# A graph layer on one core: 71 single rows per step for 40, and four edits to what the queues issue

## The chip, the cores and the metric

The kernel runs on one core of a Trainium2 chip. The metric is the time of one execution in device microseconds (us). The engines of a core run side by side and meet at semaphores: PE is the matrix engine (PEld is its loading of weights), DVE the vector engine, ACT the scalar engine, POOL the general one, and SP an engine that mostly starts DMA transfers. ACT and POOL start DMA transfers too. A name with a q (SPq, PEq) means the engine's sequencer: it waits, loads registers and issues transfers, and this is not counted as busy time. PE multiplies fp32 in two instructions, so one product of the program is two matmuls in the trace.

## The reference

There are 50,000 nodes with 128 numbers each, and 1,650,000 edges sorted by their destination. Every edge has a source, a destination and one of two types. An edge sends its source's row through the weights of its type; the messages are summed by destination; a product of the node's own row is added; then come a relu, a residual and a normalization over the 128 numbers.

```python
Xs = X[src]
m_data = Xs @ W_data.T + b_data
m_ctrl = Xs @ W_control.T + b_control
msg = jnp.where((edge_types == 0)[:, None], m_data, m_ctrl)
agg = jax.ops.segment_sum(msg, dst, num_segments=X.shape[0])
out = agg + (X @ W_self.T + b_self)
# of the whole:
x = _layernorm(x + jax.nn.relu(out), axis=-1)
```

Among the edges is one loop for every node, from the node to itself. Sum and product can change places, so the kernel first sums the source rows by destination and type and then multiplies the sums by the weights.

## The kernel before

**Blocks.** The edges are cut into blocks in their order. A block has Q = 2 steps. A step has R = 12 columns of 128 edges, whose source rows POOL fetches with one indirect DMA each (a *gather*, line 477); F = 42 *left-out* edges, which take the places of loops in those columns (a loop's row need not be fetched, since the node's own row is there anyway); and S = 40 *single rows*, which SP and ACT fetch with one plain transfer of 512 bytes each (`TURNS = (20, 20)`, SP's and ACT's share of a step). That makes 2 x (1,536 + 42 + 40) = 3,236 edges a block and NBLK = 510 blocks; the first and the last are "plain" and have neither left-out edges nor single rows. Ten blocks are a *group* (GB), whose lists of edge numbers are loaded together.

**Work for a block b**, in the order of the program's loop (lines 614 to 664). The loop goes through four *passes* (q = 0 to 3) of six columns each. The order on every engine is written out by hand; each engine works through its own instructions in this order and waits where a semaphore tells it to.

- `window(b + 3)` loads the transposed rows xT of a block's 112 destination nodes (line 406). Every BASES = 5 blocks SP loads five numbers into registers first (line 400): the first node of each block.
- `load_edges(g + 1)`, once a group: seven transfers on SP (lines 165, 170, 174).
- `products` (496): a pass waits until its six gathers have landed, then PE multiplies each 128 rows by a one-hot matrix oh. The gathers go into a ring of ten slots (`SLOTS`) of one pass each, so POOL may run ten passes ahead of PE and then waits for it (line 477).
- At the end of a step, `rows_fetched` makes PE wait (line 460, once a block, for both queues' semaphores) for the single rows of the block, and line 502 multiplies them. They lie in a ring of four blocks (`ROW_SLOTS`).
- `single_rows(b + 2, part)` issues the rows of the block after next, in two parts (q = 0 and 1). Each part first loads its 20 byte offsets into registers (`TENSOR_LOAD`, line 446), on SP and ACT each, and then issues 20 transfers (line 451), each after a MOVE of its register. The offsets are made by DVE in `offsets` (435).
- `add`, `begin_sums`, `moments`, `onehot` (412), `counts` (420), `fill` (lines 316 to 338) and `left_out_matrix` are DVE's part. `fill(b + 5)` puts left-out edges into the places of loops; `left_out_columns` (345) is PE's wait for it.
- `layer(b - 1)` (531 to 535) multiplies the finished sums by the weights; `moments`, `root` (ACT, 551), `store` (DVE, 557 and 559) and `store_rows` (SP, 563) normalize and write the block out.

Of the kernel before, what the change touches and what calls it, by code (L numbers as in the profile page):

```python
# [23 lines left out]
N = 50000  # L24
D = 128
ROW = 4 * D
E = 1650000
P = 128
# [8 lines left out]
Q = 2  # L37
PASS = 6
B = 112
C = R * Q  # L40
F = 42
TURNS = (20, 20)
S = sum(TURNS)
LOADS = 2
X = Q * S
R1 = R + 1
C1 = Q * R1
SIZES = [P] * R
SIZE = sum(SIZES)
CE = Q * SIZE  # L50
BE = CE + Q * F + X
NBLK = 2 + (E - CE) // BE
REST = E - CE - (NBLK - 2) * BE
REST_ROWS = [min(n, max(0, REST - q * SIZE - sum(SIZES[:r]))) for q in range(Q) for r, n in enumerate(SIZES)]
# [2 lines left out]
GB = 10  # L57
GROUPS = -(-NBLK // GB)
GC = GB * C1
# [17 lines left out]
assert NB * BLOCKS == N and G * BGROUPS == BLOCKS and (QB * P) % G == 0 and NCH < BIG  # L77
TBL = GROUPS * GB
GS = GB * Q


def plain(b):
# [5 lines left out]
    return bass.AP(tensor=ap.tensor, offset=ap.offset, ap=[[0, n], *ap.ap])  # L88


def straight(ctx, tc, c, x, x_t, src_t, dst_t, etype_t, src_f, dst_f, etype_f, src_x, dst_first, first_p, out):

# [20 lines left out]
    stp = ctx.enter_context(tc.tile_pool(name="stp", bufs=3))  # L113
# [5 lines left out]

    ctx.enter_context(tc.manual_schedule())  # L120
    idx0 = keep.tile([P, C1], I32, name="idx0")
    nc.sync.dma_start(idx0, src_t[:, :C1])


    num = keep.tile([P, 2 * W], F32, name="num")
# [5 lines left out]
    lists = [small[:, 2 * W + F + i * FILL:][:, :FILL] for i in range(2)]  # L131
# [7 lines left out]
                            base=0, channel_multiplier=-1)  # L139
# [11 lines left out]
    bias = keep.tile([3, D], F32, name="bias")  # L151
# [3 lines left out]
    loads = {}  # L155
# [7 lines left out]
    def load_edges(g):  # L163
        t = eds.tile([1, GB * X], I32, name="one_g")
        nc.sync.dma_start(t, src_x[None, g * GB * X:(g + 1) * GB * X])
        one_g[g] = t
        loads[g] = {}
# [224 lines left out]
    bys, pcs, zs, pls, bases, ats, ys = {}, {}, {}, {}, {}, {}, {}  # L392
    ohs, cnts, accs, xTs, pos, hs, mvs, sds, os_ = {}, {}, {}, {}, {}, {}, {}, {}, {}

    BASES = 5

    def window(b):
        if b % BASES == 0:
            n = min(BASES, NBLK - b)
            _, regs = nc.values_load_multi_w_load_instructions(  # L400
                base_i[0:1, b:b + n], engines=[SP], min_val=0, max_val=N - B,
                skip_runtime_bounds_check_because="it was clamped to this")
            bases.update({b + i: at for i, at in enumerate(regs)})
        at = bases[b]
        xT = stp.tile([P, B], F32, name="xT", bufs=5)
        nc.sync.dma_start(xT, x_t[:, bass.ds(at, B)])  # L406
        xTs[b] = xT

    def onehot(b):
# [20 lines left out]
    def offsets(b):  # L430

        if not plain(b):
            g, i = divmod(b, GB)
            ats[b] = stp.tile([1, X], I32, name="at_x", bufs=AHEAD + 2)
            nc.vector.tensor_scalar(ats[b], one_g[g][:, i * X:(i + 1) * X], float(ROW), None, op0=ALU.mult)

    def single_rows(b, part):

        if part == 0:
            ys[b] = stp.tile([S, Q, D], F32, name="yx", bufs=ROW_SLOTS)  # L440
        both = []
        for j, (eng, dma) in enumerate(((SP, nc.sync), (ACT, nc.scalar))):
            n = Q * TURNS[j]
            k0, k1 = part * n // LOADS, (part + 1) * n // LOADS
            at = Q * sum(TURNS[:j])
            _, rows = nc.values_load_multi_w_load_instructions(ats[b][0:1, at + k0:at + k1], engines=[eng], **RANGE)  # L446
            both.append([(dma, fetched[j][b % ROW_SLOTS], *divmod(k0 + k, TURNS[j]), sum(TURNS[:j]), row)
                         for k, row in enumerate(rows)])
        for pair in zip_longest(*both):
            for dma, sem, q, k, at, row in filter(None, pair):  # L450
                copy = dma.dma_start(ys[b][at + k:at + k + 1, q, :].bitcast(U8), x_bytes[:, bass.ds(row, ROW)])  # L451
# [84 lines left out]
        pos[b] = both  # L536

    def moments(b):
        h = stp.tile([B, D], F32, name="h")
# [5 lines left out]
        mv = stp.tile([B, 2], F32, name="mv")  # L545
        nc.vector.bn_aggr(mv, st)
        hs[b], mvs[b] = h, mv
# [6 lines left out]
    def store(b):  # L554
        mv = mvs.pop(b)
        rstd = stp.tile([B, 1], F32, name="rstd")
        nc.vector.reciprocal(rstd, sds.pop(b))
        o = stp.tile([B, D], F32, name="o")
        nc.vector.tensor_scalar(o, hs.pop(b), mv[:, 0:1], rstd, op0=ALU.subtract, op1=ALU.mult)
        os_[b] = o  # L560

    def store_rows(b):
        nc.sync.dma_start(out[bass.ds(bases.pop(b), B), :], os_.pop(b))  # L563

    def find_bad():

# [47 lines left out]
    for b in range(NBLK + 1):  # L614
        if b == NBLK - 1:
            find_bad()
        if b + 3 < NBLK:
            window(b + 3)
        g, i = divmod(b, GB)
        if i == 0 and g + 1 < GROUPS:  # L620
            load_edges(g + 1)
        if i == 3 and g + 1 < GROUPS:
            spread_out(g + 1)
        if i == 4 and g + 1 < GROUPS:
            spread_in(g + 1)
        if b > 0:
            add(b - 1, steps_of(b - 1)[-1])
        if b < NBLK:
            begin_sums(b)
        last = steps_of(b)[-1:]  # L630
        for q, (step, ks) in enumerate(passes_of(b)):
            if ks:
                products(b, step, ks)
            if q == 0 and b > 0:
                layer(b - 1)
            if q == 1:
                left_out_numbers(b + 1)
# [12 lines left out]
            if q == 1 and b + AHEAD < NBLK:  # L650
                counts(b + AHEAD)
            if q == 2 and i == 2 and g + 1 < GROUPS:
                columns(g + 1)
            if q == 2:
                left_out_rows(b + 1)
                if b + RAHEAD < NBLK:
                    fill(b + RAHEAD)
            if q == 3:
                left_out_matrix(b + RAHEAD)
                offsets(b + AHEAD + 1)  # L660
            if q < LOADS and not plain(b + AHEAD):
# [227 lines left out]
def gnn_resnorm(  # L889
# [1 line left out]
    tc: tile.TileContext,  # L891
    x: bass.AP,
    x_t: bass.AP,
    src_t: bass.AP,
    dst_t: bass.AP,
    etype_t: bass.AP,
    src_f: bass.AP,
    dst_f: bass.AP,
    etype_f: bass.AP,
    src_x: bass.AP,  # L900
    dst_first: bass.AP,
    first_p: bass.AP,
# [16 lines left out]
    nc = tc.nc  # L919
# [4 lines left out]
    eps = const.tile([P, 1], F32, name="eps")  # L924
# [13 lines left out]
             b_data=b_data, b_ctrl=b_ctrl, b_self=b_self)  # L938

    with ExitStack() as own:  # L940
        straight(own, tc, c, x, x_t, src_t, dst_t, etype_t, src_f, dst_f, etype_f, src_x,
                 dst_first, first_p, out)
# [10 lines left out]

# [47 lines left out]
```

## Time and profile before

| | |
|---|---|
| median of 12 runs | 18,933.21 us (18,862.37 to 18,952.98) |
| the profiled execution's own time | 18,966.55 us |
| its span, first to last instruction | 18,964.8 us |
| busy PE, DVE, POOL | 37%, 58%, 61% of the span |
| mean granted clock of PE | 0.598 |
| a gather on POOL (L477) | 944 ns busy, 12,216 and 24 of them |
| single rows on SP and on ACT (L451) | 20,320 each, 0.5 KB each |
| loads of offsets on SP (L446) | 1,016, median 1,198 ns |
| lists of a group on SP | 51 of each of seven, 3.1 to 130 KB |
| loads of matrix weights and matmuls of the single rows (L502) | 245 and 401 ns, 2,032 of each |

A line of the profile's groups reads: line, engine, operation, what it writes <- what it reads, shape, count | busy us, mean ns of one | idle time of the engine just before it, and what ended that. A line of the waits reads: who waited <- for whom: us in total, times, longest. A line of the timeline reads: start, duration, engine, line, operation, count, and in brackets the engine's idle time before it and what ended it; several of a kind in a row are merged. The view of one line of the program gives for each operation the count, the minimum, median and maximum in ns, and the first and last start. L451 is line 451 of the kernel before.

### The profile page before, as it was taken

The page shows a single profiled execution, that of the slowest core. Times are in us where ns is not written, and L with a number is a line of the kernel's source. Part 1 is how long each engine was busy: PE and PEld are TensorE (multiplying, and loading weights), DVE is VectorE, ACT ScalarE, POOL GpSimd, SP SyncE. Part 2 cuts the span into 40 slices and gives each one's busy share as a digit, 9 for nine tenths or more (in the row PEclk, how much of TensorE's full clock was granted, in tenths as well). Part 3 has the DMA queues.
Part 4 walks back from the last instruction along what each step waited for, and adds up shares of the span by engine and source line. Part 5 has one row for each costly group of instructions (what it writes and reads, how often), then busy time and mean ns, then how long its engine had stood idle before and what let it go on. Part 6 is the DMA issues. An engine that isn't in the chain of part 4 may idle for free. (4 is left out here: it accounts for less than half of the span.)

```text
span 18964.8 us, 197234 instructions
## 1 busy us (share of the span) xinstructions
PE 7104.0 (37%) x35844; PEld 6372.0 (34%) x35845; DVE 10926.6 (58%) x13994; ACT 153.5 (1%) x516; POOL 11559.9 (61%) x12250
## 2 busy tenths in 40 slices
PE   3333333333333333333333333334333333333333
PEld 2333333333333333333333333333333333333333
DVE  6555555555555555555555555555555555555554
ACT  0000000000000000000000000000000000000000
POOL 6665666656665666666666666665665666666665
PEclk6566556555655556565656565555566655566556
DMA  2211111111111211111111111111111111121111
GB/s 53 50 51 48 50 49 51 50 49 50 49 49 49 50 49 50 49 50 49 50 51 49 50 49 50 49 49 49 50 49 49 50 50 49 49 51 49 51 50 45
DMA packets 649294, 939.08 MB, mean 50 GB/s; under 512 B 327756, under 2 KB 445487, under 8 KB 648034
## 3 DMA queue, kind: packets, MB, share of 16 engines
q0 software_dynamic: 391680, 802.93, 16.8%
q1 hardware_dynamic: 215276, 112.76, 2.3%
q10 hardware_dynamic: 41078, 10.68, 0.2%
q14 instruction: 968, 7.93, 0.1%
q8 instruction: 292, 4.78, 0.1%
HBM read 895.92 MB, written 29.42 MB: 49 GB/s over the span
## 5 line engine op out<-in xcount | busy, mean ns | idle before, releaser
L477 POOL DMA_INDIRECT y<-in_x,idx x12216 | 11535.8, 944 | 7351.3 <-issue 3311.7
L496 PE MATMUL acc<-oh,y 128*128 128x120 f32 x24480 | 5044.2, 388 | 203.6 <-issue 202.4
L496 PEld LDWEIGHTS acc<-oh,y 128*128 128x128 f32 x24480 | 4774.7, 297 | 212.2 <-issue 211.7
L420 DVE TENSOR_REDUCE cnt<-oh 128x240 bf16<-128x3120 f32 x510 | 2966.9, 5818 | 0.1
L512 DVE TENSOR_TENSOR sums<-acc,sums 128x180 f32 x1020 | 352.8, 346 | 4354.2 <-PE acc L505 2086.7
L502 PE MATMUL acc<-oh,yx 40*128 40x120 f32 x2032 | 637.3, 401 | 4971.6 <-PEq L460 2960.0
L345 PE MATMUL small<-ones_b,by 128*84 128x1 bf16 x508 | 116.0, 228 | 6183.1 <-issue 3193.0
L345 PEld LDWEIGHTS <-by 128*84 128x84 bf16 x508 | 72.8, 143 | 6305.5 <-issue 3260.3
L502 PEld LDWEIGHTS acc<-oh,yx 40*128 40x128 f32 x2032 | 403.4, 245 | 5157.8 <-PEq L460 3010.8
L541 DVE COPY h<-po 112x128 f32<-112x128 f32 x510 | 148.7, 292 | 2847.3 <-remote 1410.1
L412 DVE TENSOR_TENSOR oh<-col,small 128x3120 f32<-128x3120 f32 x510 | 1719.3, 3371 | 0.0
L338 DVE TENSOR_REDUCE by<-old 128x84 bf16<-128x1092 f32 x508 | 1077.9, 2122 | 18.5 <-DVE old L335 0.9
L319 DVE TENSOR_TENSOR m<-rk,small 128x1092 f32<-128x1092 f32 x508 | 656.3, 1292 | 17.9 <-DVE small L317 0.7
L322 DVE TENSOR_TENSOR new<-m,small 128x1092 f32<-128x1092 f32 x508 | 656.1, 1291 | 17.4
L326 DVE TENSOR_REDUCE v_new<-new 128x26 f32<-128x1092 f32 x508 | 656.0, 1291 | 17.4
L335 DVE TENSOR_TENSOR old<-m,small 128x1092 f32<-128x1092 f32 x508 | 652.7, 1285 | 0.0
L535 PE MATMUL po<-wmsgT,sums 128*112 128x128 f32 x2040 | 520.5, 399 | 0.0
L535 PEld LDWEIGHTS po<-wmsgT,sums 128*112 128x112 f32 x2040 | 377.9, 255 | 108.8 <-issue 88.7
L533 PE MATMUL po<-bias,sums 3*112 3x128 f32 x1020 | 350.4, 439 | 99.4 <-DVE sums L512 64.3
L505 PE MATMUL acc<-cnt,to_row 128*128 128x60 bf16 x2040 | 272.2, 212 | 146.6 <-issue 146.1
L532 PE MATMUL po<-wselfT,xT 128*112 128x128 f32 x1020 | 313.8, 410 | 0.0
L525 DVE TENSOR_TENSOR sums<-pl,sums 128x336 f32<-128x336 f32 x508 | 258.0, 508 | 84.8 <-issue 70.9
(118 smaller groups left out, 4045.8 us busy)
## 6 DMA issues: line engine op xcount, KB each, us to landing
yx<-in_x ACTq DMA_DIRECT2D x20320, 0.5 KB
yx<-in_x SPq DMA_DIRECT2D x20320, 0.5 KB
y<-in_x,idx POOLq DMA_INDIRECT x12216
xT<-in_x_t SPq DMA_DIRECT2D x510, 56.0 KB
out<-o SPq DMA_DIRECT2D x510, 56.0 KB
vf_all<-vd SPq DMA_DIRECT2D x51, 420.0 KB
s<-in_src_t SPq DMA_DIRECT2D x51, 130.0 KB
d<-in_dst_t SPq DMA_DIRECT2D x51, 130.0 KB
```

Source lines behind the costliest of these rows:

```text
L319: nc.vector.tensor_tensor(m, rk_g[g][:, i, :, None].to_broadcast([P, C1, F]), rank_no_ps[:, None, :].to_broadcast([P, C1, F]), op=ALU.is_e ...
L322: nc.vector.tensor_tensor(new.rearrange("p (q r) f -> p q r f", r=R1), m.rearrange("p (q r) f -> p q r f", r=R1), vf.rearrange("p (q f) -> ...
L326: nc.vector.tensor_reduce(v, new, AX.X, ALU.add)
L335: nc.vector.tensor_tensor(old, m, cb[:, :, None].to_broadcast([P, C1, F]), op=ALU.mult)
L338: nc.vector.tensor_reduce(by, old.rearrange("p (q r) f -> p q f r", r=R1), AX.X, ALU.add)
L412: nc.vector.tensor_tensor(oh, col_g[g][:, i, :, None].to_broadcast([P, C1, 2 * W]), num_ps[:, None, :].to_broadcast([P, C1, 2 * W]), op=AL ...
L420: nc.vector.tensor_reduce(cnt, ohs[b].rearrange("p (q r) w -> p q w r", r=R1), AX.X, ALU.add)
L477: copy = nc.gpsimd.indirect_dma_start(out=y[:r, k % PASS, :].bitcast(U8), out_offset=None, in_=x_rows, in_offset=bass.IndirectOffsetOnAxis ...
L496: nc.tensor.matmul(acc[:, :2, :].rearrange("p t w -> p (t w)"), y[:r, k % PASS, :], ohs[b][:r, column(k), :], start=k == of_step[0], stop= ...
L502: nc.tensor.matmul(acc[:, :2, :].rearrange("p t w -> p (t w)"), ys[b][:, q, :], ohs[b][:S, q * R1 + R, :], start=False, stop=True)
L512: nc.vector.tensor_tensor(part, accs.pop((b, q)), part, op=ALU.add)
L535: nc.tensor.matmul(po, a[:, t, :B], c["wmsgT"][:, t * D:(t + 1) * D], start=False, stop=t == 1)
```

## The change

1. The single rows of a step go from 40 to 71, 35 on SP and 36 on ACT, and the left-out edges from 42 to 43. A block then has 3,300 edges. The offsets of a block are loaded in three parts of up to 32 registers for two parts of 20, issued at q = 0, 1 and 2; ACT's offsets start at a multiple of four.
2. The seven transfers of a group's lists become three: one list as before, the three lists of columns side by side in one tensor, and the three lists of left-out edges in another.
3. SP gets a block's byte offsets from DVE, which computes them once for all blocks before the loop, and no longer computes them from the node number for each transfer. The window's loads bring two numbers for each of four blocks.
4. ACT takes the root for two blocks at once; the stores of the two blocks follow it together.

```diff
-F = 42
-TURNS = (20, 20)
+F = 43
+TURNS = (35, 36)
 S = sum(TURNS)
-LOADS = 2
-X = Q * S
+LOADS = 3
+BEGIN = (0, -(-Q * TURNS[0] // 4) * 4)
+X = BEGIN[1] + -(-Q * TURNS[1] // 4) * 4
...
-BE = CE + Q * F + X
+BE = CE + Q * (F + S)
...
-        for name, a in (("s", src_t), ("d", dst_t), ("t", etype_t)):
-            t = eds.tile([P, GB, C1], I32, name=name, bufs=1)
-            nc.sync.dma_start(t.rearrange("p b c -> p (b c)"), a[:, g * GC:(g + 1) * GC])
-            loads[g][name] = t
-        for name, a in (("sf", src_f), ("df", dst_f), ("tf", etype_f)):
-            t = eds.tile([GS, F], I32, name=name, bufs=1)
-            nc.sync.dma_start(t, a[g * GS:(g + 1) * GS, :])
-            loads[g][name] = t
+        t = eds.tile([P, 3, GB, C1], I32, name="sdt", bufs=1)
+        nc.sync.dma_start(t.rearrange("p m b c -> p (m b c)"), edges_t[:, g * 3 * GC:(g + 1) * 3 * GC])
+        f = eds.tile([GS, 3, F], I32, name="sdt_f", bufs=1)
+        nc.sync.dma_start(f.rearrange("s m f -> s (m f)"), edges_f[g * GS:(g + 1) * GS, :])
+        loads[g] = {n: t[:, m] for m, n in enumerate("sdt")} | {n + "f": f[:, m] for m, n in enumerate("sdt")}
...
-    base_i = keep.tile([1, BL], I32, name="base_i")
-    nc.vector.tensor_copy(base_i, base[0:1, :, 0])
+    base_i = keep.tile([1, BL, 2], I32, name="base_i")
+    for i, size in enumerate((4, ROW)):
+        nc.vector.tensor_scalar(base_i[:, :, i], base[0:1, :, 0], float(size), None, op0=ALU.mult)
...
-    BASES = 5
+    BASES = 4
...
-        nc.sync.dma_start(xT, x_t[:, bass.ds(at, B)])
+        nc.sync.dma_start(xT.bitcast(U8), x_t_bytes[:, bass.ds(bases[b][0], 4 * B)])
...
+    def part_of(n, part):
+        return min(n, 32 * part)
...
-            k0, k1 = part * n // LOADS, (part + 1) * n // LOADS
-            at = Q * sum(TURNS[:j])
+            k0, k1 = part_of(n, part), part_of(n, part + 1)
+            at = BEGIN[j]
...
-    def root(b):
-        sd = stp.tile([B, 1], F32, name="sd")
-        nc.scalar.activation(sd, mvs[b][:, 1:2], AF.Sqrt, bias=c["eps"][:B, :])
-        sds[b] = sd
+    def pair(b):
+        return range(b // 2 * 2, b + 1) if b % 2 == 1 or b == NBLK - 1 else ()
+
+    def root(bs):
+        sd = stp.tile([B, 2], F32, name="sd")
+        nc.scalar.activation(sd[:, :len(bs)], mvs[bs[0] // 2][:, :len(bs), 1], AF.Sqrt, bias=c["eps"][:B, :])
+        sds[bs[0] // 2] = sd
...
+        for i, b in enumerate(bs):
+            o = stp.tile([B, D], F32, name="o", bufs=4)
+            nc.vector.tensor_scalar(o, hs.pop(b), mv[:, i, 0:1], rstd[:, i:i + 1], op0=ALU.subtract, op1=ALU.mult)
+            os_[b] = o
...
     def store_rows(b):
-        nc.sync.dma_start(out[bass.ds(bases.pop(b), B), :], os_.pop(b))
+        rows = out_bytes[bass.ds(bases.pop(b)[1], B * ROW)].rearrange("(p e) -> p e", e=ROW)
+        nc.sync.dma_start(rows, os_.pop(b).bitcast(U8))
...
-            if q == 1 and b > 0:
-                root(b - 1)
-            if q == 2 and b > 0:
-                store(b - 1)
+            if q == 1 and b > 0 and pair(b - 1):
+                root(pair(b - 1))
+            if q == 2 and b > 0 and pair(b - 1):
+                store(pair(b - 1))
...
             if q == 3 and b > 0:
-                store_rows(b - 1)
+                for done in pair(b - 1):
+                    store_rows(done)
```

More of the change, by code (lines that the diff above doesn't have):

```diff
@@ L79 @@
 GS = GB * Q
+CLAMPED = "it was clamped to this"
 def plain(b):
@@ L88, in row_bcast, with straight @@
     return bass.AP(tensor=ap.tensor, offset=ap.offset, ap=[[0, n], *ap.ap])
-def straight(ctx, tc, c, x, x_t, src_t, dst_t, etype_t, src_f, dst_f, etype_f, src_x, dst_first, first_p, out):
+def straight(ctx, tc, c, x, x_t, edges_t, edges_f, src_x, dst_first, first_p, out):
     nc = tc.nc
@@ L121, in straight @@
     idx0 = keep.tile([P, C1], I32, name="idx0")
-    nc.sync.dma_start(idx0, src_t[:, :C1])
+    nc.sync.dma_start(idx0, edges_t[:, :C1])
     num = keep.tile([P, 2 * W], F32, name="num")
@@ L166, in load_edges @@
         one_g[g] = t
-        loads[g] = {}
-        for name, a in (("s", src_t), ("d", dst_t), ("t", etype_t)):
-            t = eds.tile([P, GB, C1], I32, name=name, bufs=1)
-            nc.sync.dma_start(t.rearrange("p b c -> p (b c)"), a[:, g * GC:(g + 1) * GC])
-            loads[g][name] = t
-        for name, a in (("sf", src_f), ("df", dst_f), ("tf", etype_f)):
-            t = eds.tile([GS, F], I32, name=name, bufs=1)
-            nc.sync.dma_start(t, a[g * GS:(g + 1) * GS, :])
-            loads[g][name] = t
+        t = eds.tile([P, 3, GB, C1], I32, name="sdt", bufs=1)
[3 more added lines that the diff above has]
+        loads[g] = {n: t[:, m] for m, n in enumerate("sdt")} | {n + "f": f[:, m] for m, n in enumerate("sdt")}
     load_edges(0)
@@ L393, in straight @@
     ohs, cnts, accs, xTs, pos, hs, mvs, sds, os_ = {}, {}, {}, {}, {}, {}, {}, {}, {}
-    BASES = 5
+    BASES = 4
+    x_t_bytes = x_t.bitcast(U8)
+    out_bytes = out.rearrange("n d -> (n d)").bitcast(U8)
     def window(b):
@@ L400, in window @@
             _, regs = nc.values_load_multi_w_load_instructions(
[L401 to L404, printed above, removed]
+                base_i[0:1, b:b + n, :].rearrange("o b i -> o (b i)"), engines=[SP], min_val=0, max_val=(N - B) * ROW,
+                skip_runtime_bounds_check_because=CLAMPED)
+            for i in range(n):
+                at = nc.s_assert_within(regs[2 * i], 0, (N - B) * 4, skip_runtime_bounds_check_because=CLAMPED)
+                bases[b + i] = at, regs[2 * i + 1]
         xT = stp.tile([P, B], F32, name="xT", bufs=5)
-        nc.sync.dma_start(xT, x_t[:, bass.ds(at, B)])
+        nc.sync.dma_start(xT.bitcast(U8), x_t_bytes[:, bass.ds(bases[b][0], 4 * B)])
         xTs[b] = xT
@@ L538, in moments @@
     def moments(b):
-        h = stp.tile([B, D], F32, name="h")
+        h = stp.tile([B, D], F32, name="h", bufs=4)
         po = pos.pop(b)
@@ L544, in moments, with store @@
         nc.vector.bn_stats(st, h)
-        mv = stp.tile([B, 2], F32, name="mv")
+        if b % 2 == 0:
+            mvs[b // 2] = stp.tile([B, 2, 2], F32, name="mv")
+        mv = mvs[b // 2][:, b % 2, :]
         nc.vector.bn_aggr(mv, st)
-        hs[b], mvs[b] = h, mv
-    def root(b):
-        sd = stp.tile([B, 1], F32, name="sd")
-        nc.scalar.activation(sd, mvs[b][:, 1:2], AF.Sqrt, bias=c["eps"][:B, :])
-        sds[b] = sd
[L554 to L560, printed above, removed]
+        hs[b] = h
+    def pair(b):
[4 more added lines that the diff above has]
+        sds[bs[0] // 2] = sd
+    def store(bs):
+        mv = mvs.pop(bs[0] // 2)
+        rstd = stp.tile([B, 2], F32, name="rstd")
+        nc.vector.reciprocal(rstd[:, :len(bs)], sds.pop(bs[0] // 2)[:, :len(bs)])
+        for i, b in enumerate(bs):
+            o = stp.tile([B, D], F32, name="o", bufs=4)
+            nc.vector.tensor_scalar(o, hs.pop(b), mv[:, i, 0:1], rstd[:, i:i + 1], op0=ALU.subtract, op1=ALU.mult)
+            os_[b] = o
     def store_rows(b):
-        nc.sync.dma_start(out[bass.ds(bases.pop(b), B), :], os_.pop(b))
+        rows = out_bytes[bass.ds(bases.pop(b)[1], B * ROW)].rearrange("(p e) -> p e", e=ROW)
+        nc.sync.dma_start(rows, os_.pop(b).bitcast(U8))
     def find_bad():
@@ L893, in gnn_resnorm @@
     x_t: bass.AP,
[L894 to L899, printed above, removed]
+    edges_t: bass.AP,
+    edges_f: bass.AP,
     src_x: bass.AP,
@@ L940, in gnn_resnorm @@
     with ExitStack() as own:
-        straight(own, tc, c, x, x_t, src_t, dst_t, etype_t, src_f, dst_f, etype_f, src_x,
-                 dst_first, first_p, out)
+        straight(own, tc, c, x, x_t, edges_t, edges_f, src_x, dst_first, first_p, out)
     found = nc.values_load(bad, min_val=0, max_val=4 * P,
@@ L955 @@
     arrays = {k: np.ascontiguousarray(inputs[k], dtype=np.float32) for k in _FLOATS}
+    lists, fillers = [], []
     for k, pad in (("src", 0), ("dst", DST_PAD), ("edge_type_2", 0)):
@@ L975 @@
         single = steps[:, :, SIZE + F:]
-        ones[1:] = np.concatenate([single[:, :, sum(TURNS[:j]):][:, :, :n].reshape(TBL - 1, Q * n)
-                                   for j, n in enumerate(TURNS)], axis=1)
+        for j, n in enumerate(TURNS):
+            ones[1:, BEGIN[j]:BEGIN[j] + Q * n] = single[:, :, sum(TURNS[:j]):][:, :, :n].reshape(TBL - 1, Q * n)
         firsts = np.ascontiguousarray(cols[:, :, 0, 0])
-        arrays[k + "_t"] = np.ascontiguousarray(cols.reshape(TBL * C1, P).T)
-        arrays[k + "_f"] = fills.reshape(TBL * Q, F)
+        lists.append(cols.reshape(TBL * C1, P).T.reshape(P, GROUPS, GC))
+        fillers.append(fills.reshape(TBL * Q, F))
         if k == "src":
@@ L986 @@
             arrays["first_p"] = np.ascontiguousarray(both.transpose(2, 0, 1).reshape(GS, 2 * GROUPS))
+    arrays["edges_t"] = np.ascontiguousarray(np.stack(lists, axis=2).reshape(P, GROUPS * 3 * GC))
+    arrays["edges_f"] = np.ascontiguousarray(np.concatenate(fillers, axis=1))
     arrays["x_t"] = np.ascontiguousarray(arrays["x"].T)
@@ L993 @@
     with tile.TileContext(nc) as tc:
-        gnn_resnorm(tc, ap["x"], ap["x_t"], ap["src_t"], ap["dst_t"], ap["edge_type_2_t"], ap["src_f"], ap["dst_f"],
-                    ap["edge_type_2_f"], ap["src_x"], ap["dst_first"], ap["first_p"], ap["src"],
-                    ap["dst"], ap["edge_type_2"],
+        gnn_resnorm(tc, ap["x"], ap["x_t"], ap["edges_t"], ap["edges_f"], ap["src_x"], ap["dst_first"], ap["first_p"],
+                    ap["src"], ap["dst"], ap["edge_type_2"],
                     ap["L0_gnn_W_data"], ap["L0_gnn_b_data"], ap["L0_gnn_W_control"],
```

## The prediction

> **What bounds the kernel now.** I read the page first, then the waits of all engines, then SP's own waits, and last the timelines of SP, PE and POOL side by side. The page gives no engine as full:
>
> ```profile
> PE 7104.0 (37%) x35844; PEld 6372.0 (34%) x35845; DVE 10926.6 (58%) x13994; ACT 153.5 (1%) x516; POOL 11559.9 (61%) x12250
> ...
> L477 POOL DMA_INDIRECT y<-in_x,idx x12216 | 11535.8, 944 | 7351.3 <-issue 3311.7
> ...
> L502 PE MATMUL acc<-oh,yx 40*128 40x120 f32 x2032 | 637.3, 401 | 4971.6 <-PEq L460 2960.0
> ```
>
> POOL issues 24 gathers per block, one every 1.25 us (0.94 busy and 0.30 of issue), so 30.0 us of a block; a block takes 18,964.8 / 510 = 37.19 us. What holds POOL for the other 7 us is PE, through the ten slots of y, and PE itself sits in front of L502, the product with the single rows. The view of line 460 alone, PE's wait for those rows, has 508 waits with a median of 11.46 us. The waits of all engines say the same, and SP's own waits say who is late:
>
> ```profile
> PEld acc L502 <- PEq L460: 3010.8, 202, 26.0
> ...
> POOL y L477 <- PE acc L496: 1966.3, 410, 11.5
> ```
>
> ```profile
> SPq L446 <- DVE sums L512: 72.8, 74, 1.5
> SPq L301 <- DVE cb L279: 15.7, 1, 15.7
> SPq L563 <- DVE o L559: 11.1, 3, 6.8
> ```
>
> These are SP's three largest waits, 100 us in 18,965: SP is never out of work. It is not counted as busy, because issuing DMAs is not, but it is the full queue. The timeline of SP, with PE's for the same moment behind it:
>
> ```profile
> 8007.78 36.70 SPq L451 DMA_DIRECT2D yx<-in_x  x40
> 8044.74 0.34 SPq L563 DMA_DIRECT2D out<-o  x1
> 8045.32 0.36 SPq L406 DMA_DIRECT2D xT<-in_x_t  x1
> ...
> 8047.75 31.65 SPq L451 DMA_DIRECT2D yx<-in_x  x40
> ```
>
> ```profile
> 8045.55 0.50 PEld L502 LDWEIGHTS acc<-oh,yx 40*128 40x128 f32 x2 [10.52 <-PEq L460]
> ```
>
> SP ends its 40 rows at 8044.48, and PE goes on 1.1 us later after 10.52 us of waiting. Pairing every one of the 508 fences with the two queues, from the trace's records: 430 of them wait, and in all 430 SP's last row comes after ACT's, by more than a block and a half; the median from SP's last row to the end of the fence is 1.0 us. So SP's 40 rows bound the kernel, not POOL's gathers. ACT has the same 40 rows and room to spare.
>
> The price of a row is not constant, and this decides the sum. It depends on whether POOL is gathering:
>
> ```profile
> L451 SPq DMA_DIRECT2D yx<-in_x x7: 3/689/711, 8021.9 to 8031.1; - x7
> ```
>
> ```profile
> L451 SPq DMA_DIRECT2D yx<-in_x x21: 13/228/689, 11685.0 to 11694.3; - x21
> ```
>
> ```profile
> 11682.37 0.94 POOL L477 DMA_INDIRECT y<-in_x,idx  x1 [0.30 <-issue]
> 11694.85 0.94 POOL L477 DMA_INDIRECT y<-in_x,idx  x1 [11.53 <-PE acc L496]
> ```
>
> The columns are count and minimum, median, maximum in ns. Between 8021 and 8033 POOL gathers, ACT issues, and SP gets 7 rows out in 12 us. Between 11,685.5 and 11,694.5 POOL stands still for PE, and SP gets 21 rows out in 9 us. The timeline has a whole set of 40 at 11,691.70 in 16.00 us, against 36.70 above: 0.40 and 0.92 us a row, loads of the numbers included. The mean over all 508 sets is 31.5 us from first to last row, 0.79 a row; the other 5.7 us of SP's block are the first load, out, xT, the window's numbers and the lists.
>
> **The change part by part.** A block takes 3,300 edges for 3,236, so the blocks are 2 + 499 = 501 for 510, and the gathers 500 x 24 + 2 = 12,002 for 12,240. At POOL's own 1.25 us that is 297 us less, but POOL is not the bound, so alone it brings nothing.
>
> The single rows go from 40 to 70 per block on SP and from 40 to 72 on ACT. That is 30 rows more on the queue that is full. Bounds for one row: 0.40 us (the set at 11,691.70) and 0.92 (the set at 8007.78). I take 0.40, because the gathers of a block still take only 30.0 us: a block of before already lasts 37.19, so whatever is added to it is added while PE waits at L460, y's slots stay taken and POOL stands still, and that is the row measured in such a pause. 30 x 0.40 = 12.0 us. The loads are in it: before there are two loads of 20 registers per 40 rows, median 1.20 us each on SP, and after three of 32, 32 and 6 per 70.
>
> Taken from SP: four list transfers per ten blocks, medians 0.33 to 0.43 us, together 1.5 us or 0.15 per block; one register multiply each at L563 and L406, median 37 ns but 0.17 us in the mean of 510, together 0.34. Added: loads of the window's numbers, 8 registers every 4 blocks for 5 every 5, at 0.95 us each at least 0.05. I take -0.4; between the ends 0 and -0.6 it moves the total by 0.2 ms.
>
> Lying beside it: the left-out edges go from 42 to 43, so L319, L322, L326, L335 and L338 (7.28 us a block) grow by 1/42, 0.17 us on DVE; the offsets of L435 go from 80 to 144 numbers, 0.195 us now and at most 0.35 by length; the yx weights grow from 40 to 71 partitions, and L496 with 128 partitions takes 388 ns where L502 with 40 takes 401, so nothing on PE. The cover of all this is PE's wait at L460, 6,197 us in the 508 fences, 12.2 per block; without it 0.32 us x 501 would be 0.16 ms.
>
> The root for two blocks: ACT has one wait for mv fewer in two blocks, and where it remains it stands at the same place, with the second and third part of the rows of b+2 queued behind it, as before. The store of an even block moves one block later, past one set of SP's rows and one xT; its o and h have four buffers for it, and only the end of the program reads the output. DVE then makes two o in a row (0.40 us more in an odd block, that much less in an even one), ahead of the fill. On SP two out transfers follow each other, the number of them is the same on the mean. I cost this at nothing, under the same cover.
>
> Sum: 37.19 + 12.0 - 0.4 = 48.8 us; 501 x 48.8 = 24,450 us on the profiled span of 18,964.8 (its own time is 18,966.55). The last block has 2 gathers for 24, some 20 us less, and the median of the runs stands 33 us under the profiled run, 0.2%. That gives 24,400 us. About 0.2% is also what a measurement of this kernel can tell from no change.
>
> The Trainium skill, "DMA: Bandwidth & Descriptors", section "Issuing engines are not separate DMA queues", says that starting DMAs from several engines saves only the sequencer's time to start them, and that this is usually small beside the DMA. The rows above speak otherwise for 0.5 KB rows: starting them is all of SP's time, and PE goes on 1.0 us after the last start. By that rule the 30 starts would be small and the sum would be the first rival's.
>
> **The rivals.** *Faster.* What bounds a block is the work of the gathers, and SP is slow only because it has time until they let it on. Then time goes with the gathers: 12,002 x 18,964.8 / 12,240 = 18,596, less 33 is 18,560 us. For it: SP's rows slow down exactly when POOL gathers, and POOL has the most busy time of all engines. Against it: POOL's pauses end with PE, PE's with SP, and the gathers are there early, since L496 has only 203.6 us of idle time before it. The point at which it decides: 70 rows and SP's other 5.3 us fit into 37.2 us if a row costs 0.45 or less on the mean; it is 0.79 now.
>
> *ACT becomes the bound.* It has 72 rows and issued during 13,532 us of the trace (71% of the span, counting stretches without a hole over 1 us). Scaled by rows, 0.71 x 37.19 x 72 / 40 = 47.5 us a block, 23,800. That is so near that both may hold each other up; the place would be L460 with ACT's row last.
>
> *The mean price stays.* If the new rows cost what rows cost on the mean, 30 x 0.79 = 23.7, a block is 60.5 us and the time 30,300. For it: ACT's rows nearly double too and fill the pauses. Against it: there is no work for POOL in the added time.
>
> *No change.* The savings on SP would have to equal 12 us; nothing of that size is taken away.
>
> **How the numbers follow.** Forecast 0.65 at 24,400; ACT 0.13 at 23,800; mean price 0.08 at 30,300; faster 0.12 at 18,560; no change 0.02. Low end of the forecast: with ACT done, SP got 28 rows out in the 16 us from 11,696 although POOL was gathering, 0.57 a row; 30 us of gathers then hold 52.6 rows, the remaining 17.4 cost 7.0, with 5.3 for the rest 42.3 us, 21,200. High end: half of the new rows at 0.92, 37.19 + 13.8 + 6.0 - 0.4 = 56.6 us, 28,350. With a little on both for the unknown mix, 20,800 to 28,500 leaves out the faster case and the mean price, 0.20. Slower is 0.65 + 0.13 + 0.08 = 0.86.
>
> **What would show it.** Right: SP's waits stay near nothing, its sets of 70 rows take 35 to 50 us, L460's median grows to 20 us or more, POOL's idle time before L477 roughly doubles while its busy time falls 2%. Step by step: rows in a pause of POOL at 0.32 to 0.40 us (the price), ACT's last row before SP's (else the second rival), DVE's idle time up by about 10 us a block (the cover). Wrong: L460 waits shorter than now, or a span near 18.6 ms with POOL's pauses as they are; then SP had room that its timeline does not show.

## The result, and the profile after

The changed kernel takes 24,971.48 us (median of 8 runs, 24,944.33 to 24,996.51). The kernel before, run beside it, takes 18,919.32 us (34 runs, 18,862.37 to 18,984.09). The ratio is 1.32, with a 95% interval of 1.3185 to 1.3214: a third slower. The forecast of 24,400 us is 2.3% low and lies on the right side; the profiled execution of after took 24,964.79 us, with a span of 24,963.1. One thing is needed to read the experiments: they ran in four sessions, in three of which the kernel before took 15.32 to 15.33 ms and in one 19.22 ms, and each kernel is compared only with the runs of before in its own session.

The page of after, engines and two costliest groups that answer to those shown of before:

```profile
PE 6844.3 (27%) x35177; PEld 6351.5 (25%) x35178; DVE 10792.8 (43%) x13519; ACT 77.3 (0%) x257; POOL 11344.3 (45%) x12012
...
L483 POOL DMA_INDIRECT y<-in_x,idx x12000 | 11341.0, 945 | 13523.3 <-PE acc L502 8881.5
...
L508 PE MATMUL acc<-oh,yx 71*128 71x120 f32 x1996 | 596.0, 392 | 12700.2 <-PEq L466 12407.9
```

No engine does more work than before; POOL and PE are busy for less time. What grew is the idle time in front of the gathers (7,351.3 to 13,523.3 us, line 477 is now 483) and in front of the product with the single rows (4,971.6 to 12,700.2, line 502 is now 508). The waits of all engines give the same two, each more than four times as large as before:

```profile
PEld acc L508 <- PEq L466: 12521.1, 469, 39.6
...
POOL y L483 <- PE acc L502: 8898.9, 573, 24.3
```

The view of line 466 alone, PE's wait for the single rows (line 460 before). The columns are minimum, median and maximum in ns:

```profile
L466 PEldq EVENT_SEMAPHORE  x499: 51/30032/41397, 113.5 to 24917.0; - x167
```

Its median goes from 11.46 to 30.03 us. SP's own waits, the two largest:

```profile
SPq L577 <- DMA out<-o: 342.3, 251, 2.8
SPq L452 <- DVE sums L518: 87.4, 51, 2.1
```

Together they are 430 us of 24,963: SP is still never out of work. The first of them is nearly new (5.1 us in the trace of before), and the prediction had costed it at nothing: of a pair of out transfers the second waits for the first. SP's timeline shows where it stands, and the timelines of PE and POOL for the same moment show what follows from it:

```profile
12004.58 46.17 SPq L457 DMA_DIRECT2D yx<-in_x  x70
12050.92 2.15 SPq L577 DMA_DIRECT2D out<-o  x2
12053.22 0.38 SPq L408 DMA_DIRECT2D xT<-in_x_t  x1
12055.82 45.87 SPq L457 DMA_DIRECT2D yx<-in_x  x70
```

```profile
12052.13 0.79 PE L508 MATMUL acc<-oh,yx 71*128 71x120 f32 x2 [26.83 <-PEq L466]
```

```profile
12038.63 0.94 POOL L483 DMA_INDIRECT y<-in_x,idx  x1 [0.30 <-issue]
12056.36 0.94 POOL L483 DMA_INDIRECT y<-in_x,idx  x1 [16.79 <-PE acc L502]
```

SP's set of rows ends at 12,050.75. PE, which had waited 26.83 us, goes on 1.4 us later; POOL, whose ring of ten passes was full, goes on 4.2 us after PE, when the first slot is free. SP meanwhile is at its next set. It goes round through a set of 70 rows and what lies between two sets, with no waits but those few above.

The price of a row in and out of POOL's pause, from the view of line 457 on SP:

```profile
L457 SPq DMA_DIRECT2D yx<-in_x x11: 2/12/713, 12012.6 to 12022.5; - x11
```

```profile
L457 SPq DMA_DIRECT2D yx<-in_x x24: 3/228/684, 12040.6 to 12049.9; - x24
```

While POOL gathers, 11 rows take 9.9 us, 0.9 each; in the pause from 12,039.6 to 12,056.4, 24 rows take 9.3 us, 0.39 each. In the trace's records, 495 of the 499 fences wait, and in all 495 SP's last row comes after ACT's, by 89 us on the median and 21 at least. (In the trace of before it is 61 us on the median and 38 at least; the "more than a block and a half" of the prediction is the median, not every fence.) SP's set takes 45.59 us on the mean (0.651 a row) and the stretch between sets 4.34; a block is 24,963.1 / 501 = 49.83 us. That set and stretch add up to a block is so by definition; that SP bounds it is read from its waits, which are 430 us in all.

### The profile page after: what moved, and what is told of

Same layout as the page of the kernel before. It is cut to its first block, busy times and chain, and to the rows that moved or that the text cites. A ratio compares the mean times of both kernels' runs of the same rounds, so it can differ in the third digit from the quotient of the medians.

```text
span 24963.1 us, 254178 instructions
## 1 busy us (share of the span) xinstructions
PE 6844.3 (27%) x35177; PEld 6351.5 (25%) x35178; DVE 10792.8 (43%) x13519; ACT 77.3 (0%) x257; POOL 11344.3 (45%) x12012
## 3 DMA queue, kind: packets, MB, share of 16 engines
q0 software_dynamic: 384080, 787.32, 12.5%
## 4 chain that ended last, share of the span: by engine, by line
SPq 60%; issue 36%; DMA 2%; DVE 1%; PE 1%; PEld 0%; PEldq 0%; another core or an unknown queue 0%; ACT 0%; DVEq 0%; ACTq 0%
SPq L457 50%; SPq L452 8%; DMA yx<-in_x 1%; DMA out<-o 1%; SPq L408 1%; PE acc L508 1%; SPq L401 0%; DVE cnt L422 0%; PE acc L502 0%; SPq L577 0%; DVE by L337 0%; PE pl L363 0%; DVE sums L518 0%; PEld acc L502 0%; PE pl L360 0%
## 5 line engine op out<-in xcount | busy, mean ns | idle before, releaser
L483 POOL DMA_INDIRECT y<-in_x,idx x12000 | 11341.0, 945 | 13523.3 <-PE acc L502 8881.5
L502 PE MATMUL acc<-oh,y 128*128 128x120 f32 x24004 | 5015.8, 394 | 15.4 <-issue 15.3
L502 PEld LDWEIGHTS acc<-oh,y 128*128 128x128 f32 x24004 | 4777.0, 304 | 19.2 <-issue 19.1
L508 PE MATMUL acc<-oh,yx 71*128 71x120 f32 x1996 | 596.0, 392 | 12700.2 <-PEq L466 12407.9
L508 PEld LDWEIGHTS acc<-oh,yx 71*128 71x128 f32 x1996 | 421.0, 263 | 12820.2 <-PEq L466 12521.1
L344 PE MATMUL small<-ones_b,by 128*86 128x1 bf16 x499 | 115.4, 231 | 5113.9 <-issue 2802.8
L337 DVE TENSOR_REDUCE by<-old 128x86 bf16<-128x1118 f32 x499 | 1080.5, 2165 | 17.9 <-DVE old L334 0.7
L318 DVE TENSOR_TENSOR m<-rk,small 128x1118 f32<-128x1118 f32 x499 | 658.8, 1320 | 17.4 <-DVE small L316 0.5
L321 DVE TENSOR_TENSOR new<-m,small 128x1118 f32<-128x1118 f32 x499 | 658.8, 1320 | 17.1
L325 DVE TENSOR_REDUCE v_new<-new 128x26 f32<-128x1118 f32 x499 | 657.7, 1318 | 17.1
L334 DVE TENSOR_TENSOR old<-m,small 128x1118 f32<-128x1118 f32 x499 | 654.0, 1311 | 0.0
L511 PEld LDWEIGHTS <-to_row 128*128 128x128 bf16 x2002 | 265.1, 132 | 30.9 <-issue 2.3
```

The costliest lines, as they stand in the source:

```text
L318: nc.vector.tensor_tensor(m, rk_g[g][:, i, :, None].to_broadcast([P, C1, F]), rank_no_ps[:, None, :].to_broadcast([P, C1, F]), op=ALU.is_e ...
L321: nc.vector.tensor_tensor(new.rearrange("p (q r) f -> p q r f", r=R1), m.rearrange("p (q r) f -> p q r f", r=R1), vf.rearrange("p (q f) -> ...
L325: nc.vector.tensor_reduce(v, new, AX.X, ALU.add)
L337: nc.vector.tensor_reduce(by, old.rearrange("p (q r) f -> p q f r", r=R1), AX.X, ALU.add)
L483: copy = nc.gpsimd.indirect_dma_start(out=y[:r, k % PASS, :].bitcast(U8), out_offset=None, in_=x_rows, in_offset=bass.IndirectOffsetOnAxis ...
L502: nc.tensor.matmul(acc[:, :2, :].rearrange("p t w -> p (t w)"), y[:r, k % PASS, :], ohs[b][:r, column(k), :], start=k == of_step[0], stop= ...
```

## Experiments

**The theory.** A block takes as long as the slowest of three: POOL's 24 gathers (24 x 1.25 = 30.0 us), SP's set of rows with the rest of SP's queue, and ACT's queue with its rows and the root. The change puts SP far above POOL. The rivals: edits 2 to 4 carry a part of the loss (the paired root and store above all); the 142 rows of a block meet a limit that both queues share, so that it doesn't matter who issues them; ACT's queue is the one that is late. The expectations of the first four runs were written before a session at 15.3 ms had been seen. "A 15-ms session" and "the 19-ms session" are named below by the time of the kernel before in them.

**Edits 2 to 4 alone.** Rows, left-out edges and the number of loads go back to before (the loads bring 32 and 8 offsets, not 20 and 20); all else is the changed kernel.

```diff
-F = 43
-TURNS = (35, 36)
+F = 42
+TURNS = (20, 20)
-LOADS = 3
+LOADS = 2
```

> The changed kernel with the rows, left-out edges and blocks of before (20 and 20 rows a step, 42 left-out edges, 510 blocks); offsets are loaded in parts of 32 and 8. Theory (SP's rows set the block): the four edits are worth little. SP loses 0.4 us a block and gains up to 0.7 where the second of two stores waits for the first; a block stays at 36.6 to 37.9 us, 18,650 to 19,350 us in all. Rival (one of the edits, above all the paired stores and roots, made the added time): a block near 48 us or more, over 24,000 us.

Measured: 15,347.6 us, before beside it 15,322.89; ratio 1.001 (0.9994 to 1.0026). The page's line of the gathers, and the view of line 466:

```profile
L483 POOL DMA_INDIRECT y<-in_x,idx x12216 | 11573.6, 947 | 3737.8 <-issue 3572.3
```

```profile
L466 PEldq EVENT_SEMAPHORE  x508: 51/51/51, 107.4 to 15300.2; - x170
```

The idle time before the gathers is POOL's own issue, 0.3 us each, and PE never waits for single rows. POOL is full: 510 x 30.0 = 15,300 us. SP's set of 40 takes 14.05 us here, 0.351 a row, and with the rest of its queue it stays far under 30. So in a 15-ms session like this one the row's price is less than half of the 0.796 in the trace of before above, and the edits, in the shade of the gathers, are worth nothing that can be measured. What they cost where SP is the bound this run can't tell; for the pairing it is asked again below.

**The rows alone.** The kernel before, with 35 and 36 rows, three loads and 43 left-out edges, and none of edits 2 to 4.

```diff
-F = 42
-TURNS = (20, 20)
+F = 43
+TURNS = (35, 36)
-LOADS = 2
-X = Q * S
+LOADS = 3
+BEGIN = (0, -(-Q * TURNS[0] // 4) * 4)
+X = BEGIN[1] + -(-Q * TURNS[1] // 4) * 4
...
-            k0, k1 = part * n // LOADS, (part + 1) * n // LOADS
-            at = Q * sum(TURNS[:j])
+            k0, k1 = min(n, 32 * part), min(n, 32 * (part + 1))
+            at = BEGIN[j]
...
```

> The kernel before with 35 and 36 rows a step, 43 left-out edges and loads of up to 32, and no other edit (seven lists, offsets computed on SP, a root for every block). Theory: 30 more rows on SP at 0.43 us each make the block 37.1 + 12.9 = 50.0 us, times 501 some 25,000 us (24,600 to 25,500), SP's last row after ACT's in every wait. Rival (the edits made the added time): 18,600 us, by the fewer gathers.

Measured, in the same session: 15,844.15 us, ratio 1.0334 (1.032 to 1.0349). SP's timeline and the wait for single rows:

```profile
8023.57 26.40 SPq L452 DMA_DIRECT2D yx<-in_x  x70
```

```profile
L461 PEldq EVENT_SEMAPHORE  x499: 51/9329/21686, 108.2 to 15807.2; - x167
```

A set of 70 takes 26.44 us on the mean, 0.378 a row, and 5.21 lie between sets: 31.65 us, against POOL's 30.0. But the mean hides where the time is lost. SP's largest wait, and its timeline at the lists of a group:

```profile
SPq L175 <- DMA out<-o: 536.7, 49, 12.3
```

```profile
8296.17 0.34 SPq L175 DMA_DIRECT2D df<-in_dst_f  x1
8306.87 0.28 SPq L175 DMA_DIRECT2D tf<-in_edge_type_f  x1
```

Once in ten blocks the last of the seven list transfers waits some 11 us until an earlier out transfer has landed, and SP's round with the lists in it takes 44.3 us on the mean; the other nine take 30.2, almost POOL's own time. These waits are 537 us in all, and the whole loss is 521. So 71 rows bring SP up to POOL's time here, and what is lost beyond it stands at the wait in the seven lists, which edit 2 makes three; a run without that wait was not made. The size of the loss hangs on the session too: 1.6 us a block at 0.38 us a row, and 12.6 at 0.65.

**The whole change in a 15-ms session.** The changed kernel as it is, in the fourth session.

> The changed kernel as it is, sent once more for a chip where the kernel before takes 15.3 ms. There SP needs 70 x 0.38 + 4.5 = 31 us and ACT 72 x 0.38 + 4 = 31.4 us, both just over POOL's 30.0: 15,500 to 15,900 us, 1.01 to 1.04 of before, if SP's queue decides as in the run with the rows alone (1.033). Rival (the paired root waits behind ACT's rows, and DVE for it at L569, as in the run with 40 rows a step on ACT): 16,000 us and more. On a chip where before takes 19 ms: 1.31 to 1.32 of before.

Measured: 15,871.29 us, before 15,323.25; ratio 1.0358 (1.0341 to 1.0376). SP's timeline, its largest wait, and the wait for single rows:

```profile
8000.38 26.28 SPq L457 DMA_DIRECT2D yx<-in_x  x70
8026.83 4.81 SPq L577 DMA_DIRECT2D out<-o  x2
```

```profile
SPq L577 <- DMA out<-o: 844.2, 252, 5.7
```

```profile
L466 PEldq EVENT_SEMAPHORE  x499: 51/10215/25303, 105.8 to 15824.8; - x167
```

A set takes 26.35 us and 5.36 lie between sets, 31.71 in all, and SP's last row comes after ACT's in all 485 fences that wait. The rows alone stood at 1.0334 in another session; the intervals of the two meet (1.0341 to 1.0349), so what edits 2 to 4 add, if anything, is some 0.2%. SP's queue no longer has the wait in the lists (537 / 499 = 1.1 us a block) and the multiplies, and loses 844 / 499 = 1.7 us a block to the second out transfer; the two about cancel (5.36 between sets for 5.21). Without the second out's wait SP's block would be 31.7 - 1.7 = 30.0 us, which is POOL's: an estimate. So whether 71 rows with the fewer lists and one out transfer per block lose anything at all in such a session is not shown.

**Rows moved from SP to ACT.** The same number of rows, 31 a step on SP and 40 on ACT. If SP's own issuing is the limit, this brings its set under POOL's 30 us; if both queues share a limit, nothing changes.

```diff
-TURNS = (35, 36)
+TURNS = (31, 40)
```

> The changed kernel with 31 rows a step on SP and 40 on ACT; the same 71 rows, blocks and gathers. Theory (SP's own rows): 8 rows fewer on SP at 0.43 us, block 49.85 - 3.4 = 46.4 us, some 23,250 us (22,900 to 23,700); SP's last row still after ACT's, ACT's set grows from 39.0 to about 42 us. Rival (all 142 rows of a block share one limit, whichever queue issues them): no change, 24,970 us within 1%. Rival (ACT is as near the bound as SP): no gain, with ACT's row last in L466's waits.

> Again 31 rows a step on SP and 40 on ACT with the same 71, 501 blocks and gathers. Where the kernel before takes 19 ms: the theory (SP's own rows) takes 8 x 0.45 = 3.6 us off the changed kernel's block of 50 us, 46.5 us and 23,300 us (1.22 to 1.24 times before), as the run with 31 and 32 rows had it. Rival (142 rows share one limit whichever queue issues them): 1.30 to 1.32 times before, as the changed kernel. Where the kernel before takes 15.3 ms: 16,400 us again, with ACT as the late queue.

Measured: 16,407.71 us and 16,411.4, ratios 1.0703 (1.0688 to 1.0718) and 1.0709 (1.0694 to 1.0725); slower than the changed kernel. ACT's timeline and two lines of the waits, from the first of the two:

```profile
8010.85 0.30 ACT L563 ACTIVATE sd<-mv,eps 112x2 f32<-112x2 f32 x1 [65.39 <-issue]
8013.13 63.00 ACTq L457 DMA_DIRECT2D yx<-in_x  x160
8076.24 0.30 ACT L563 ACTIVATE sd<-mv,eps 112x2 f32<-112x2 f32 x1 [65.09 <-issue]
```

```profile
PEld L344 <- DVE by L337: 9637.3, 499, 32.8
...
DVE rstd L569 <- ACT sd L563: 3600.2, 251, 27.1
```

```profile
ACT sd L563 <- issue: 16156.7, 248, 65.9
```

PE waits for no single row any more (the median at line 466 is 0.05 us), and SP, at 22.81 us a set, waits for others. But ACT has become the bound: 80 rows take 30.28 us and 2.51 lie between sets, 32.79 a block, and by the last line ACT's roots had, in nearly all of the run, nothing in front of them but ACT's own issuing. The root stands in the same queue: it begins when the rows in front of it are issued, DVE waits up to 27.1 us for it, and the filling of the blocks (line 337), which PE needs, stands behind that wait on DVE. The same 142 rows cost SP 0.368 us each and ACT 0.378, much as before the move (0.376 and 0.380). So the limit is each queue's own and not shared, here at least; and the others feel a full ACT through the root that they wait for.

**Half the rows.** The kernel before with ten rows a step on each queue, 517 blocks and 12,392 gathers in place of 12,240.

```diff
-TURNS = (20, 20)
+TURNS = (10, 10)
```

> The kernel before with 10 and 10 rows a step, so 517 blocks and 12,392 gathers. Theory: SP needs 20 x 0.79 + 5.4 = 21 us a block and is no longer the bound; POOL's 24 gathers of 1.25 us and its short waits set it, 30 to 32.5 us a block, 15,500 to 16,800 us, waits for single rows (L460) near nothing. Rival (the work of the gathers sets a block and SP only fills the time): 1.2% more gathers, 18,919 x 12,392 / 12,240 = 19,150 us.

> Again the kernel before with 10 and 10 rows a step, 517 blocks. Where the kernel before takes 19 ms: the theory gives SP 20 x 0.8 to 1.1 us + 5.4 = 22 to 28 us, under POOL's 30; 30 to 32 us a block, 15,500 to 16,600 us, 0.81 to 0.87 of before, faster than both kernels; L460's waits near nothing. Rival (gathers as such are slower on such a chip): 517/510 of before, 19,450 us. Where the kernel before takes 15.3 ms: 15,530 us again, 1.013 of before.

> The kernel before with 10 and 10 rows a step, sent once more, for a chip where the kernel before takes 19 ms (the earlier two went to chips where it takes 15.3). There the theory gives SP 20 x 0.8 to 1.1 us + 5.4 = 22 to 28 us, under POOL's 30; 30 to 32 us a block, 15,500 to 16,600 us, 0.81 to 0.87 of before, faster than both kernels. Rival (gathers as such are slower on such a chip): 517/510 of before, 19,450 us. On a chip where before takes 15.3 ms: 15,530 us, 1.013 of before.

Measured: 15,532.89, 15,522.2 and 15,517.29 us in three sessions, ratios 1.0131 (1.0115 to 1.0148), 1.0129 (1.0115 to 1.0143) and 1.0127 (1.011 to 1.0144). The gathers' line of the first:

```profile
L477 POOL DMA_INDIRECT y<-in_x,idx x12384 | 11701.9, 945 | 3782.7 <-issue 3637.8
```

POOL is full as in the first experiment, and the time goes with the gathers: 12,392 / 12,240 = 1.0124. Where the gathers bound, single rows are worth having, for each takes the place of a gathered one. This kernel was meant for a session in which before takes 19 ms, where by the theory it would be the fastest of all (20 x 0.8 + 5.4 = 21 us on SP, under POOL's 30); all three of its sessions were of the other kind, so that stays an estimate.

**Both kernels again, before at 19.2 ms.** In the second session:

> The changed kernel as it is. The theory now has two terms for a block, and the longer one counts: POOL's 24 gathers at 1.25 us, 30.0 us, and SP's set of rows plus about 5 us for the rest of its queue. Only the price of a row differs between chips. On a chip where the kernel before takes 18.9 ms (0.8 us a row at 40, 0.65 at 70): 24,970 us again, block 49.9. On a chip where it takes 15.3 ms (0.35 to 0.38 us a row): SP 26.4 + 4.5 = 31 us, just over POOL's 30, so 15,500 to 15,900 us, 1 to 4% slower, SP's last row the late one. Rival (ACT with 72 rows and the root between them is the late queue here): 16,000 us and more, with DVE waiting for the root at L569 as in the run with 40 rows a step on ACT.

> The kernel before as it is, for a trace beside the others. On a chip where it takes 15.3 ms: SP's set of 40 rows 14 us, L460's waits near nothing, POOL without pauses, a block 30.0 us. On a chip where it takes 18.9 ms: the trace of before again, SP's set 32 us, block 37.1.

Measured: after 25,250.7 us, ratio 1.3141 (1.3106 to 1.3176); before, traced once more, 19,261.96. All readings return: SP's set 46.02 us after and 32.36 before, and SP's last row after ACT's in all 496 and all 432 waiting fences. If every idle time of POOL over 0.45 us counts as a pause, a row on SP takes 0.89 us while POOL gathers and 0.60 in pauses in this trace of before (0.86 and 0.60 in the first), and 0.90 and 0.45 in that of after (0.89 and 0.44).

**One root per block again.** The changed kernel with root, store and out transfer for every block, as before. It asks what the pairing costs where SP is the bound.

```diff
...
     def pair(b):
-        return range(b // 2 * 2, b + 1) if b % 2 == 1 or b == NBLK - 1 else ()
+        return range(b, b + 1)
...
-        nc.scalar.activation(sd[:, :len(bs)], mvs[bs[0] // 2][:, :len(bs), 1], AF.Sqrt, bias=c["eps"][:B, :])
-        sds[bs[0] // 2] = sd
+        nc.scalar.activation(sd[:, :len(bs)], mvs[bs[0]][:, :len(bs), 1], AF.Sqrt, bias=c["eps"][:B, :])
+        sds[bs[0]] = sd
...
```

> The changed kernel with a root, a store and an out transfer for every block, as before. Theory: the second of two out transfers no longer waits for the first (342 us in 251 waits of the changed kernel's trace, 0.68 us a block on SP), one ACTIVATE more per two blocks on ACT. Where SP sets the block, 0.5 to 0.9 us less of it: 250 to 450 us under the changed kernel, on either kind of chip. Rival (that wait lies beside other work of SP or is only moved): within 0.3% of the changed kernel. Rival (the root waits more often behind ACT's rows, and DVE for it): slower.

Measured: 25,138.11 us, ratio 1.3082 (1.3047 to 1.3116), 112 us or 0.4% under the changed kernel of the same session; the runs of the two don't overlap (25,085 to 25,153 and 25,190 to 25,269), the intervals do. SP's waits, first in the changed kernel run beside it, then with one root per block:

```profile
SPq L577 <- DMA out<-o: 339.2, 251, 2.7
SPq L452 <- DVE sums L518: 87.1, 51, 2.0
```

```profile
SPq L452 <- DVE sums L518: 519.2, 440, 2.0
...
SPq L576 <- DMA out<-o: 4.9, 4, 1.2
```

The wait of the second out transfer is gone, as expected, but a larger one comes in its place: line 452, the load of a part's offsets, now waits more often for DVE, 519 us for 87. Little was won. The pairing is about 0.4% of the time here, and the loss of a third stays without it.

**Eight rows fewer on each queue.** The changed kernel with 31 and 32 rows a step, 503 blocks.

```diff
-TURNS = (35, 36)
+TURNS = (31, 32)
```

> The changed kernel with 31 rows a step on SP and 32 on ACT: 63 a step, 503 blocks, 12,062 gathers or so. Theory: where a row costs 0.37 us, SP needs 62 x 0.37 + 4.5 = 27.5 us and ACT 64 x 0.38 + 4 = 28.3, both under POOL's 30.0, so POOL sets the block and the fewer gathers count: 503/510 of the kernel before, 15,090 to 15,200 us, faster than both kernels. Where a row costs 0.65 us: 62 rows are 8 fewer than 70, 3.4 us less, 46.5 us a block, 23,300 us. Rival (DVE's wait for paired roots decides on a quick chip): 15,500 us and more.

Measured: 23,461.72 us, ratio 1.2213 (1.218 to 1.2246). SP is last in all 496 fences that wait, with a set of 42.23 us and 4.42 between. The view of line 466:

```profile
L466 PEldq EVENT_SEMAPHORE  x501: 51/26952/39247, 114.6 to 23385.1; - x167
```

Blocks of 46.58 us in place of 50.28 are 3.70 us for 8 rows, 0.46 us a row: the price at the margin, measured from another side, and the same as from before to after. ACT had eight rows fewer too, so this run alone doesn't tell SP's own limit from a shared one.

## Why the prediction was right, by its own steps

**What bounds.** Right. SP's queue was full before and is full after, SP's last row ends every wait at PE's fence, and ACT's is ahead by 89 us, so the second rival falls. POOL was never the bound in the runs that were forecast: its work fell by 2% (11,559.9 to 11,344.3 us) and the time rose by a third.

**Thirty rows at 0.40 us.** The mechanism is right, the size too small, and the price came from a row that shows something else. SP's set went from 31.82 to 45.59 us, 13.8 for 30 rows, 0.46 each. POOL's pauses, counted as above, went from 7.9 to 20.5 us a block, 12.6 more, which is what the block grew by, so the added time does lie in pauses. Of the 30 rows, 27 fall into pauses and add 10.2 us, 0.38 each, close to the forecast; but the part of a set that lies beside the gathers grew as well, by three rows and 3.5 us. That was put at nothing, and it is why the term is 1.8 us a block short, 0.9 ms. The prediction took its 0.40 from this set of before and called it a row measured in a pause:

```profile
11691.70 16.00 SPq L451 DMA_DIRECT2D yx<-in_x  x40
```

POOL's lines that it shows say otherwise: the pause ended at 11,694.85, and 13 of these 16 us lie beside gathers, in a stretch in which ACT issued nothing. The rows it shows in the pause itself, 21 in 9 us, are 0.43 each. That 0.40 was near the truth is in part luck.

**Minus 0.4 us for lists and multiplies.** Too small as well, in the other direction. What lies between two sets went from 5.41 to 4.34 us, 1.1 less. By the trace's records of SP's instructions there, the lists gave 0.25 us a block (0.15 forecast), and out and xT with what stands in front of them went from 3.04 to 1.74 although the second out's wait of 0.69 is now in it: 2.0 us less, for which 0.34 was forecast. Against this, a block's first load, now of 32 registers for 20, went from 1.18 to 2.06 us. In the timeline of after, out and xT stand in a pause of POOL; that they cost less for this reason was not tested.

**The pairing at nothing.** Wrong in its reason, harmless in its size. There was a wait behind the words "on SP two out transfers follow each other": 342.3 us, 0.69 a block. The run with one root per block got back 112 us.

**The sum.** The terms as measured, 37.2 (set and gap of before) + 13.8 - 1.1, give 49.9 us by the way they are defined, against 48.8 forecast; a block measured 49.83. The rows were 1.8 us short and the savings 0.7, and these misses of opposite sign leave the 2.3%: that it is so little is luck.

**The signs.** A set of 70 at 35 to 50 us: 45.6. The fence's median at 20 us or more: 30.0. POOL's idle time doubled: a factor of 1.84. A row in POOL's pauses at 0.32 to 0.40 us: 0.44 over all pauses, so this sign was missed by a little. DVE's idle time up by 10 us a block: the block grew by 12.6 with DVE's work per block the same (10,926.6 / 510 and 10,792.8 / 501 us, 21.4 and 21.5), so by about 12.5; the cover on DVE was there.

**The rival that said faster** named its own point: 0.45 us a row. In the sessions where a row costs 0.38 the change is still slower, by 3.6%, because POOL's 30.0 us and not the 37.2 of the trace are then what 70 rows and the rest must fit into, and they take 31.7, the second out's wait of 1.7 included. The forecast of a third would have been far off there: it holds for sessions with the row prices of the trace it was read from. The Trainium skill's statement in "DMA: Bandwidth & Descriptors", section "Issuing engines are not separate DMA queues", that the time to start a DMA is usually small relative to the DMA itself, is no guide for these rows of 0.5 KB in either kind of session: starting 70 of them is 26 or 46 us of a block, and in the latter PE goes on 1.3 us (median) after the last start.

**Open.** Moving rows to ACT, half the rows, the rows alone, and edits 2 and 3 by themselves were not measured where a row costs 0.65 us; there the cause rests on the traces and on the run with 31 and 32 rows. Nor are the queues independent there: in the trace of after a row on SP in POOL's pauses takes 0.43 us while ACT issues too and 0.34 while it does not (0.62 and 0.37 in that of before), so a part of the price goes with what the other queue does. None of the runs beat the kernel before. With 31 and 32 rows and the price of the 15-ms sessions, SP's block would be 62 x 0.376 + 5.4 = 28.7 us, under POOL's 30.0, and 503 x 30.0 = 15,090 us, 1.5% under before: an estimate, not run there.

## What to carry to other kernels

An engine that the profile counts as nearly idle can be the bound: look for the queue that waits for nothing, divide its issuing time by what it issues, and put that price, at the margin and with the loads it needs, against the time of the next full engine. Here a plain transfer of 512 bytes cost its queue 0.35 to 0.8 us, and in the 15-ms sessions 20 rows a step took 1.3% more than 40, and 71 took 3% more: rows pay off as long as SP's queue stays under POOL's gathers. Before taking work off a full queue by moving it to another, see how near that other queue is to full and what else stands in it: with 80 rows ACT's queue took 32.8 us a block where SP's had taken 31.7, and DVE and PE felt it through ACT's root.

## What the runs showed of the hardware

**The same kernel at 15.3 and at 18.9 to 19.2 ms.** The kernel before took 15,320 to 15,356 us in three sessions and 19,166 to 19,278 in one (18,862 to 18,984 beside the changed kernel). It does not go with the number of the chip: on the chip numbered 7 it took 19.2 ms in one session and 15.3 in another. It is not the clock of PE: 0.598 was granted in the trace of before at 19.0 ms, and less, 0.538, in that of edits 2 to 4 alone at 15.4. It is not the gathers either: POOL issues one every 1.25 us in every trace. What differs is the price of starting a transfer on SP and ACT. SP's MOVEs in front of the rows, first in the trace of after and then in that of the same kernel in a 15-ms session:

```profile
L457 SPq MOVE yx<-in_x x34930: 1/29/1476, 27.2 to 24938.9; - x200
```

```profile
L457 SPq MOVE yx<-in_x x34930: 29/29/29, 27.1 to 15846.8; - x200
```

Where before takes 18.9 ms or more, single MOVEs and transfers take 700 ns and more at times, and a row on SP costs 0.86 to 0.95 us on the mean while POOL gathers and 0.44 to 0.60 in its pauses. In the 15-ms sessions every such MOVE takes 29 to 40 ns, and a row costs 0.35 to 0.38 us in sets of 40 and more, with POOL gathering nearly all the time. Why a session is of the one or the other kind was not found; no kernel with fewer gathers was run, so that the gathers cause the stalls is only seen side by side.

**Records that lag.** In the traces of the 19-ms session, and in those of before and after shown first, 10 to 18% of ACT's single rows have a packet that begins before the recorded start of the instruction that issued it, by up to 2.7 us. In the 15-ms sessions there is none; the packet begins 0.84 us or more after the instruction. This would fit a recording of instructions that is backed up and holds up the queues with it, but no run tests that.

**The landing of rows.** In the run with the rows alone, ACT's rows began to move 7.4 us after they were issued on the median, against about 1 us in the other traces, and the page puts 13% of the chain that ended last on these transfers. SP's rows were late too: PE's fence ends 10.9 us after SP's last row was issued, on the median, against 1.0 and 1.3 us in the traces of before and after. In most blocks SP's queue ran on during that time, but once in ten blocks it stood still for the landing of an out transfer (the 537 us at line 175 above), and that is about the whole loss of this run. Why the landings were late there was not found.
